# A list-scheduled graph-network kernel: GpSimd instructions wait for VectorE instructions that the plan puts ahead of them

## The chip, the cores and the metric

The kernel runs on one core of a Trainium2 chip, in float32 throughout. A core has five engines that run their own queues in order: TensorE (PE in the profile, its weight loads PEld), VectorE (DVE), ScalarE (ACT), GpSimd (POOL) and SyncE (SP), which here issues all DMAs. [...] The metric is the device time of one execution in microseconds; a profile's span is the time between the first and last instruction of the profiled execution.

## The reference

128 graphs of 128 nodes with 512 features go through four layers. Each layer adds its result to its input and normalises every row. `adj` is a 128x128 matrix for each graph.

```python
x = layernorm(x + relu(An @ x @ W0 + b0))                    # layer 0; An = dh * (adj + I) * dh
q, k = split(x @ Wqk.T);  v = x @ Wv.T                       # layer 1
w = softmax_over_nodes(sum((q @ k.T) / 8 * adj, -1))
x = layernorm(x + w * v)
agg = adj @ x / max(deg, 1e-6)                               # layer 2
x = layernorm(x + relu(concat(x, agg) @ W2.T))
x = layernorm(x + An @ (x @ W3 + b3))                        # layer 3
```

`dh` is the inverse root of a row sum of `adj + I`, and `deg` a row sum of `adj`.

## The kernel before, in words

Four graphs make a tile (`G = 4`), so there are 32 tiles; the four layers of a tile are spread over several rounds of the main loop, so that at any time layer 0 of one tile, layer 1 of the same, and layers 2 and 3 of the tile before are in work (lines 889 to 905). `begin` (line 856) holds the first rounds, with the weights' sums between them, and lines 907 to 916 the last tile, in pairs of graphs.

Each 512x512 product (`project`, line 526; `l1_out`, line 729) is cut into two by two blocks and computed with seven block products instead of eight: B11, T1, B21, T2, B22, T3, T4. The left operands of T1, T2, B22 and T3 are sums of blocks, which `left_sums` (line 503) computes with four instructions of 128x512: s1, s2, the overwritten block a21, and s4. In the profile these are agg0s, agg2s, agg3s, xT1s, xT2s and, for a21, agg or xT. They run on GpSimd, but for some of `begin`. TensorE's products read them.

VectorE adds the products in PSUM to blocks in SBUF (u_o, s_o, v) and to `x`, takes the rows' means and variances (bno, mvo; bnv, mvv), prepares the adjacency of a later tile (deg, dh, ana, anT), and computes layer 1's scores: `l1_scores` (line 695) ends with four scr instructions, which give w; `l1_softmax` turns w on TensorE (p_w), takes the exponentials on ScalarE (e), scales them on VectorE, and turns them back (p_ws). `norm_stats` (line 626) sends mean and variance through GpSimd (rstd, with a power, then mr) and ScalarE (nmr, then x in place). The last norm is `norm_last` (line 601). Turned copies of x (xT1, xT2) go through DRAM and a VectorE transpose in the steady tiles, and over TensorE (p_xT, from xT1y or xT2y) in the first and last.

None of this is emitted where it is written. `Recorder` turns each call into an `Op` of a `Plan`, with a duration from `estimate` (line 292). `schedule` (line 197) then simulates the five engines: TensorE's order is the recorded one; each other engine takes, of its ready ops, the one whose latest allowed start is smallest. An op with `port` set (all of GpSimd's, and VectorE's with two large SBUF inputs, lines 303 to 308) may not start before the previous op with `port` has ended (lines 236 and 250). `emit` (line 268) then issues all ops in the planned order. That order binds each engine's own queue. Between two engines only the data's own dependencies become semaphore waits; the planned order of a GpSimd and a VectorE op with `port` is otherwise not enforced.

All instructions of the plan carry line 271 in the profile, so they are told apart by their tiles' names.

Of the kernel before, what the change touches and what calls it, by code (L numbers as in the profile page):

```python
# [32 lines left out]
class Ref:  # L33


    def __init__(self, tile_, steps, idx, quads):
        self.tile, self.steps, self.idx, self.quads = tile_, steps, idx, quads
# [83 lines left out]
class Op:  # L121
    def __init__(self, engine):
        self.engine, self.dur, self.lat, self.size, self.port, self.calls, self.preds, self.succs = engine, 0, 0, 0, False, [], set(), []
        self.last, self.start, self.end = float("inf"), None, None


class Plan:
# [2 lines left out]

    ENGINES = ("tensor", "vector", "scalar", "gpsimd", "sync")
    HOP = 200
    LAND, FLIGHT = 1600, 9
    HEAD, BUS = 40000, (62, 95)

    def __init__(self, nc, est):
        self.nc, self.est, self.ops, self.tags, self.group, self.dram = nc, est, [], {}, None, None
        for e in self.ENGINES:  # L140
            setattr(self, e, Recorder(self, e))

# [54 lines left out]
    def schedule(self):  # L197
        number = {op: i for i, op in enumerate(self.ops)}
        for (_, tag, bufs), tiles in self.tags.items():
            used = []  # L200
            for t in sorted((t for t in tiles if t.ops), key=lambda t: number[t.ops[0]]):
                if len(used) == bufs:
                    old = used.pop(min(range(bufs), key=lambda i: number[used[i].ops[-1]]))
                    assert number[old.ops[-1]] < number[t.ops[0]], (tag, bufs)
                    for op in t.ops:
                        if op.preds.isdisjoint(t.ops):
                            op.preds.update(old.ops)
                used.append(t)
        now = 0
        for op in self.ops:  # L210
            assert all(number[p] < number[op] for p in op.preds)
            for p in op.preds:
                p.succs.append(op)
            if op.engine == "tensor":
                op.last = now
                now += op.dur
        for op in reversed(self.ops):
            due = min([s.last - self.hop(op, s) for s in op.succs], default=now)
            op.last = min(op.last, due - op.dur)
        queue = {e: [] for e in self.ENGINES}  # L220
        waiting = {op: len(op.preds) for op in self.ops}
        free, bus, port = dict.fromkeys(self.ENGINES, 0), 0, 0
        pe = [op for op in self.ops if op.engine == "tensor"]
        for op in self.ops:
            if not op.preds:
                queue[op.engine].append((0, number[op], op))
        done, landed = [], []
        while len(done) < len(self.ops):
            best = None
            for e in self.ENGINES:  # L230
                q = queue[e]
                if e == "tensor":
                    q = [c for c in q if c[2] is pe[0]]
                if not q:
                    continue
                q = [(max(c[0], port if c[2].port else 0),) + c[1:] for c in q]
                at = max(free[e], min(c[0] for c in q))
                pick = min((c for c in q if c[0] <= at), key=lambda c: (c[2].last, c[1]))
                for c in q:
                    if at < c[0] < at + pick[2].dur and c[2].last < at + pick[2].dur and c[2].last < pick[2].last:  # L240
                        pick, at = c, c[0]
                if best is None or at < best[0]:
                    best = at, e, pick[2]
            at, e, op = best
            queue[e] = [c for c in queue[e] if c[2] is not op]
            if e == "sync" and len(landed) >= self.FLIGHT:
                at = max(at, landed[-self.FLIGHT])
            op.start, op.end = at, at + op.dur
            free[e] = op.end
            if op.port:  # L250
                port = op.end
            if e == "sync":
                bus = max(bus, op.end + self.LAND) + op.size / self.BUS[at > self.HEAD]
                op.lat = max(op.lat, bus - op.end)
                landed.append(op.end + op.lat)
            if e == "tensor":
                pe.pop(0)
            done.append(op)
            for s in op.succs:
                waiting[s] -= 1  # L260
                if not waiting[s]:
                    queue[s.engine].append((max(p.end + self.hop(p, s) for p in s.preds), number[s], s))
        return done

    def hop(self, p, s):
        return p.lat if p.engine == s.engine and p.engine != "sync" else p.lat + self.HOP

    def emit(self):
        for op in self.schedule():
            for method, args, kw in op.calls:  # L270
                getattr(getattr(self.nc, op.engine), method)(  # L271
                    *[v.real() if isinstance(v, Ref) else v for v in args],
                    **{k: v.real() if isinstance(v, Ref) else v for k, v in kw.items()})


class Recorder:
# [35 lines left out]
def kernel(  # L312
# [10 lines left out]
    b3: bass.AP,  # L323
    out: bass.AP,
):
    nc = Plan(tc.nc, estimate)
    B = x.shape[0]
    NT = B // G
    last = NT - 1
# [55 lines left out]
    p = ps_t.tile([P, C, P], FP, tag="pt", name="p_warm")  # L385
# [563 lines left out]
```

## Time and profile before

| | |
|---|---|
| time, median of 4 runs | 2452.12 us (2450.71 to 2452.63) |
| profiled execution: its own time, its span | 2451.62 us, 2449.8 us |
| granted TensorE clock over the span | 1.0 |
| TensorE busy (matmul; weight load) | 2438.0 us; 2090.9 us |
| VectorE, ScalarE, GpSimd busy | 1715.1 us; 995.5 us; 1314.5 us |
| distance of one tile to the next, from 194 to 2237 us | 75.6 us |
| a left sum on GpSimd, 128x512 (xT1s) | 1.27 us |
| rstd's power on GpSimd, 128x2 (rstdo) | 0.72 us |

A group of instructions is named by the tile that it writes and the tiles that it reads; `128x512 f32 x31` is the shape and the count. A row of the groups gives busy time and mean ns of one, then the engine's idle time before them and what ended it. A row of the waits gives the sum in us, how often, and the longest. A row of the timeline gives start and duration in us; in brackets stands the idle time before it and its releaser. "issue" means that the profile shows nothing that the engine waited for.

### The profile page before, as it was taken

To read this page: it belongs to the slowest core of one execution; us is meant where nothing else is said; L and a number is where in the kernel's file an instruction comes from. 1 tells how busy PE (TensorE), PEld (TensorE's weight loads), DVE (VectorE), ACT (ScalarE), POOL (GpSimd) and SP (SyncE) were. 2 spreads that over 40 slices of the span, in tenths; PEclk is the share of its full clock that TensorE was granted. 3 is DMA by queue.
4 is the path that set the end of the run, shared out by engine and by line. 5 is a ranking of instruction groups with operands and counts; after the bars stand their busy time and mean duration, and the time that the engine had idled before them with its cause. 6 is when DMAs were issued, how large, how long until landed. Compare 5 with 4: busy or idle time off the path is not lost.

```text
span 2449.8 us, 35470 instructions
## 1 busy us (share of the span) xinstructions
PE 2438.0 (100%) x12462; PEld 2090.9 (85%) x12462; DVE 1715.1 (70%) x3396; ACT 995.5 (41%) x2117; POOL 1314.5 (54%) x1580
## 2 busy tenths in 40 slices
PE   9999999999999999999999999999999999999998
PEld 8888888888888888888888888888888888888887
DVE  7767766677666777667776667767677676777666
ACT  4334343443434444344443444333444334443345
POOL 6464555555555555555455554645546455555543
PEclk9999999999999999999999999999999999999999
DMA  5133233442424423244332443233442333433220
GB/s 181 48 99 104 73 108 91 125 125 58 115 78 125 125 67 110 77 122 125 82 96 82 117 125 104 73 99 104 121 123 63 96 103 117 125 74 96 67 80 35
DMA packets 393266, 241.15 MB, mean 98 GB/s; under 512 B 140416, under 2 KB 358016, under 8 KB 393088
## 3 DMA queue, kind: packets, MB, share of 16 engines
q1 hardware_dynamic: 393088, 238.88, 35.3%
q8 instruction: 99, 1.62, 0.3%
q14 instruction: 79, 0.65, 0.1%
HBM read 126.62 MB, written 112.20 MB: 97 GB/s over the span
## 4 chain that ended last, share of the span: by engine, by line
PE 98%; DVE 1%; POOL 0%; issue 0%; ACT 0%; POOLq 0%; DVEq 0%
PE p_o L271 63%; PE p_v L271 20%; PE p_agg L271 14%; PE p_sc L271 1%; PE p_w L271 0%; DVE x L271 0%; PE p_warm L271 0%; PE p_ws L271 0%; PE p_xT L271 0%; DVE u_o L271 0%; POOL xT1s L271 0%; POOL rstdo L271 0%; POOL w2x_sb L271 0%; DVE ana L271 0%; DVE bno L271 0%
## 5 line engine op out<-in xcount | busy, mean ns | idle before, releaser
L271 PE MATMUL p_o<-w_sb,agg 128*128 128x256 f32 x2048 | 471.4, 380 | 0.9 <-DVE u_o L271 0.9
L271 PEld LDWEIGHTS p_o<-w_sb,agg 128*128 128x128 f32 x2048 | 386.8, 190 | 52.1 <-DVE u_o L271 0.9
L271 ACT COPY agg<-p_agg 128x512 f32<-128x512 f32 (+1 forms) x415 | 226.0, 552 | 407.3 <-PE p_agg L271 407.1
L271 PE MATMUL p_v<-wv_sb,xT 128*128 128x320 f32 x1024 | 291.7, 433 | 0.1
L271 PE MATMUL p_o<-w2x_sb,xT 128*128 128x256 f32 x1024 | 263.1, 380 | 1.0 <-ACT xT L271 1.0
L271 DVE TENSOR_TENSOR v<-p_v,v 128x320 f32<-128x320 f32 x316 | 154.4, 489 | 155.9 <-PE p_v L271 155.4
L271 PE MATMUL p_o<-w2a_sb,agg 128*128 128x256 f32 x1024 | 262.9, 379 | 0.0
L271 PEld LDWEIGHTS p_v<-wv_sb,xT 128*128 128x128 f32 x1024 | 192.3, 190 | 76.3 <-ACT xT L271 0.6
L271 PEld LDWEIGHTS p_agg<-anT,x 128*128 128x128 f32 x2048 | 238.8, 192 | 7.0 <-DVE anT L271 0.6
L271 DVE TENSOR_TENSOR u_o<-p_o,u_o 128x512 f32<-128x512 f32 (+1 forms) x196 | 129.2, 671 | 162.0 <-PE p_o L271 160.4
L271 PE MATMUL p_agg<-anT,x 128*128 128x128 f32 x2048 | 239.4, 275 | 0.3 <-DVE anT L271 0.3
L271 PEld LDWEIGHTS p_o<-w2x_sb,xT 128*128 128x128 f32 x1024 | 194.5, 190 | 30.5 <-ACT xT L271 1.4
L271 PE MATMUL p_v<-wv_sb,xT1s 128*128 128x320 f32 x768 | 217.6, 433 | 1.1 <-POOL xT1s L271 1.1
L271 PEld LDWEIGHTS p_o<-w2a_sb,agg 128*128 128x128 f32 x1024 | 194.9, 190 | 26.1
L271 POOL TENSOR_SCALAR rstdo<-mvo 128x2 f32<-128x2 f32 (+1 forms) x131 | 35.7, 273 | 321.2 <-DVE mvo L271 318.8
L271 PE MATMUL p_o<-w2x_sb,xT2s 128*128 128x256 f32 x768 | 197.2, 379 | 0.0
L271 PE MATMUL p_o<-w2a_sb,agg2s 128*128 128x256 f32 x768 | 197.2, 379 | 0.0
L271 ACT ACTIVATE x<-x,nmro,rstdo 128x512 f32<-128x512 f32 x256 | 195.0, 807 | 3.4
L271 PEld LDWEIGHTS p_v<-wv_sb,xT1s 128*128 128x128 f32 x768 | 145.8, 190 | 58.9 <-POOL xT1s L271 2.0
L271 PE MATMUL p_o<-w_sb,agg0s 128*128 128x256 f32 x768 | 180.9, 380 | 0.0
L271 PE MATMUL p_o<-w_sb,agg3s 128*128 128x256 f32 x744 | 173.9, 384 | 0.0
L271 DVE BATCH_NORM_STATS2 bno<-x 128x6 f32<-128x512 f32 x258 | 170.4, 683 | 3.9
(146 smaller groups left out, 4256.9 us busy)
## 6 DMA issues: line engine op xcount, KB each, us to landing
x<-in_x_dram SPq DMA_DIRECT2D x31, 1024.0 KB, 6.6
out_dram<-x SPq DMA_DIRECT2D x31, 1024.0 KB, 5.2
xT2s<-x SPq DMA_DIRECT2D x120, 256.0 KB, 2.8
xT2y<-xT2s SPq DMA_DIRECT2D x240, 128.0 KB, 2.7
xT1s<-x SPq DMA_DIRECT2D x120, 256.0 KB, 2.5
xT1y<-xT1s SPq DMA_DIRECT2D x240, 128.0 KB, 3.1
sa<-ana SPq DMA_DIRECT2D x120, 128.0 KB, 3.1
ya<-sa SPq DMA_DIRECT2D x120, 128.0 KB, 3.2
```

The source lines that it names most:

```text
L271: getattr(getattr(self.nc, op.engine), method)(*[v.real() if isinstance(v, Ref) else v for v in args], **{k: v.real() if isinstance(v, Ref ...
```

## The change

When `schedule` places a GpSimd op (all of them have `port`), and the last op with `port` that it placed is VectorE's, and the GpSimd op's own inputs would be ready earlier than 500 ns after that VectorE op's planned end, the GpSimd op gets `after` set to the VectorE op. `emit` then adds a dependency, so that the last instruction of the GpSimd op waits on a semaphore for the last instruction of the VectorE op. The plan's times and its order are computed as before. The plan keeps the tile context (`tc`) for this.

```diff
@@ class Op
-        self.last, self.start, self.end = float("inf"), None, None
+        self.last, self.start, self.end, self.after = float("inf"), None, None, None
@@ class Plan
-    HOP = 200
+    HOP, CLOSE = 200, 500
...
-    def __init__(self, nc, est):
-        self.nc, self.est, self.ops, self.tags, self.group, self.dram = nc, est, [], {}, None, None
+    def __init__(self, tc, est):
+        self.tc, self.nc, self.est, self.ops, self.tags, self.group, self.dram = tc, tc.nc, est, [], {}, None, None
@@ schedule
-        free, bus, port = dict.fromkeys(self.ENGINES, 0), 0, 0
+        free, bus, port, owner = dict.fromkeys(self.ENGINES, 0), 0, 0, None
...
             if op.port:
-                port = op.end
+                ready = max((p.end + self.hop(p, op) for p in op.preds), default=0)
+                if e == "gpsimd" and owner is not None and owner.engine == "vector" and ready < port + self.CLOSE:
+                    op.after = owner
+                port, owner = op.end, op
@@ emit
-                getattr(getattr(self.nc, op.engine), method)(
+                op.ins = getattr(getattr(self.nc, op.engine), method)(
                     *[v.real() if isinstance(v, Ref) else v for v in args],
-                    **{k: v.real() if isinstance(v, Ref) else v for k, v in kw.items()})
+                    **{k: v.real() if isinstance(v, Ref) else v for k, v in kw.items()}).ins
+            if op.after is not None:
+                self.tc.add_manual_dep(op.ins, op.after.ins.name, mybir.DependencyInfo(
+                    mybir.DependencyClass.Sync, mybir.DependencyReason.DATA))
...
-    nc = Plan(tc.nc, estimate)
+    nc = Plan(tc, estimate)
```

## The prediction

> **What bounds the kernel now.** I read the page first: busy shares, then the chain that ended last.
>
> ```profile
> span 2449.8 us, 35470 instructions
> PE 2438.0 (100%) x12462; PEld 2090.9 (85%) x12462; DVE 1715.1 (70%) x3396; ACT 995.5 (41%) x2117; POOL 1314.5 (54%) x1580
> PE 98%; DVE 1%; POOL 0%; issue 0%; ACT 0%; POOLq 0%; DVEq 0%
> ```
>
> TensorE is the bound from end to end; GpSimd is half idle. So the change can only gain where TensorE waits, and only lose where a later GpSimd result makes TensorE wait. Next I read who waited for whom on TensorE. The matmul side waited under 5 us in all. The weight-load side shows two repeated gaps without a named releaser:
>
> ```profile
> PEld p_ws L271 <- issue: 10.7, 32, 0.4
> PEld p_w L271 <- issue: 9.6, 27, 0.4
> ```
>
> The timeline of weight loads tells them apart. A usual tile, then the second-last:
>
> ```profile
> 1251.52 1.60 PEld L271 LDWEIGHTS p_o<-w_sb,agg 128*128 128x128 f32 x8
> 1253.47 0.08 PEld L271 LDWEIGHTS p_w<-ident,w 128*4 128x4 f32 x1 [0.35 <-issue]
> 1253.50 0.30 PEld L271 LDWEIGHTS p_o<-w_sb,agg3s 128*128 128x128 f32 x2
> ```
>
> ```profile
> 2310.41 1.60 PEld L271 LDWEIGHTS p_o<-w_sb,agg 128*128 128x128 f32 x8
> 2312.03 0.09 PEld L271 LDWEIGHTS p_w<-ident,w 128*4 128x4 f32 x1
> 2312.25 0.52 PEld L271 LDWEIGHTS p_o<-w_sb,agg3s 128*128 128x128 f32 x3
> ```
>
> From the eight loads' start to the agg3s load is 1.98 us in the first and 1.84 us in the second. So the p_w gap is a real stall worth some 0.14 us, of which TensorE makes good the rest (0.33 lost, 0.19 recovered). The p_ws gap is there in every tile, and e has been ready 0.4 to 0.8 us by then: that one is TensorE's own. What p_w waits for stands on VectorE and GpSimd in the same microseconds:
>
> ```profile
> 1250.70 1.28 POOL L271 TENSOR_TENSOR agg3s<-agg 128x512 f32<-128x512 f32 x1 [5.70 <-ACT agg L271]
> ```
>
> ```profile
> 1250.78 1.75 DVE L271 TENSOR_TENSOR ana<-ana,d 128x512 f32<-128x512 f32 x1
> 1252.46 0.27 DVE L271 SCALAR_TENSOR_TENSOR scr<-p_sc,dmn,v 128x64 f32<-128x64 f32 x1
> 1253.28 0.08 DVE L271 DVE_READ_ACCUMULATOR scr<-p_sc,dmn,v 128x1 f32 x1
> ```
>
> The last scr ends at 1253.35, and p_w loads 0.12 us later; that distance is the same in 28 tiles (27 in the row above, one under another releaser). scr is late because ana in front of it takes 1.75 us. The groups by form show what it costs otherwise:
>
> ```profile
> L271 DVE TENSOR_TENSOR ana<-ana,d 128x512 f32<-128x512 f32 x32 | 36.9, 1154 | 1.2 <-POOL d L271 1.2
> L271 DVE TENSOR_TENSOR ana<-ana,rdeg 128x512 f32<-128x512 f32 x32 | 22.8, 712 | 0.1
> ```
>
> **What the skill says.** The Trainium skill, "SBUF — State Buffer", section "Who interferes with whom": a VectorE instruction with two SBUF inputs contends with a GpSimd instruction that reads SBUF, and whoever issues first holds the shared pair for its whole instruction. The trace agrees: GpSimd started 0.08 us ahead and VectorE's 0.7 us became 1.75. The same section says TensorE and ScalarE wait on no one; TensorE's products kept their spacing through both spans. "Perfetto Trace Analysis", section "GPSIMD Engine Instruction", warns that GpSimd's spans are unreliable; here successive starts of left sums are 1.34 to 1.37 us apart with spans of 1.27, so I use the spans and add 0.08 between.
>
> **The change, part by part.** (1) No instruction moves on any of the five queues, DMAs included. The planner's arithmetic for starts is the same; only `after` and its waits are new. (2) In the emitted program 344 GpSimd instructions wait for a later VectorE instruction than before. Laid on the trace, 56 of these VectorE instructions had ended before GpSimd started, so those waits cost nothing; 288 had not, with ends 0.05 to 5 us after GpSimd's start, half of them 1 to 2 us. (3) GpSimd gets 110 more semaphore instructions, where two waits meet. No row prices one. I take nothing; bound: not below nothing, and up to one GpSimd hop, 0.08 us, each, 9 us in all on an engine that idles 1135 us.
>
> What matters is how late GpSimd's results come against how early they are needed. I followed each result through its consumers to the TensorE product it feeds, taking the idle time on the way as its slack.
>
> *Steady tiles, the gain.* agg3s<-agg now goes behind ana. ana runs 1250.78 to 1251.49 (0.71), about 1.0 us earlier than now. The first scr then starts when p_sc is done (1251.77), the fourth ends at 1252.66, and p_w may load at 1252.78; TensorE gets there at 1253.14. The stall is gone: 28 tiles by 0.145 us (load to load around p_w, 0.760 + 0.033 us with the stall, 0.432 + 0.216 in the four tiles without) = **4.0 us gained**.
>
> *Steady tiles, the delays.* agg3s<-agg starts at 1251.58 (a VectorE end reaches GpSimd in 0.09), 0.88 us late, ends at 1252.86; its product now comes at 1253.36: 0.45 us to spare. Behind it on the queue, agg<-agg waits for ana<-ana,rdeg: it ends at about 1259.2 instead of 1256.7, 2.5 late with 3.9 of slack. rs<-rs,d is 3 late with 8 of slack. rstdv, which feeds ScalarE's normalisation and then the transposing DMAs on SyncE, ends 1.3 to 2.1 late with 2.1 to 2.9 of slack: some 0.75 to spare. In turn the late agg<-agg blocks one x<-v,ws,x until 1259.2; VectorE's next reading of p_o is then 0.2 late with 0.55 of slack. Before agg3s, and again before xT1s, GpSimd idles for microseconds, so a delay doesn't pass into the next tile. Cost: nothing, under cover of 0.45 us or more. Were the cover gone, each 0.1 us would cost 3 us over 30 tiles.
>
> *Opening.* Slack is small here:
>
> ```profile
> 33.40 1.26 POOL L271 TENSOR_TENSOR agg<-agg 128x512 f32<-128x512 f32 x1
> 36.18 0.29 POOL L271 TENSOR_TENSOR mro<-mvo,rstdo 128x2 f32<-128x2 f32 x1
> 45.68 1.26 POOL L271 TENSOR_TENSOR xT1s<-xT 128x512 f32<-128x512 f32 x1
> ```
>
> ```profile
> 36.50 0.20 ACT L271 ACTIVATE nmro<-mro 128x2 f32<-128x2 f32 x1 [6.63 <-POOL mro L271]
> 38.16 1.12 ACT L271 COPY xT1y<-x 128x512 f32<-128x512 f32 x2
> ```
>
> The agg<-agg here waits for x<-s_o,x, now ending at 35.9: it runs 36.0 to 37.3, and the three rstdo/mro steps behind it end at 38.6 instead of 36.5: 2.2 late, slack 0.46. So p_xT<-xT1y stalls TensorE 1.7 us. Later steps catch up in part: w2x_sb behind s_o delays xT1s only from 45.68 to some 46.7, and TensorE, which waited 0.66 us there already, resumes at 48.0 instead of 47.0. **1.0 us lost.** From there the opening's chains run relative to TensorE again.
>
> *End.* mrv<-mvv,rstdv (2392.55) waits for four x<-v,ws,x: 1.0 late with no slack, but TensorE's 0.68 us wait five steps on (xT, 2397.5) takes most of it: 0.3 lost. agg30s moves x<-s_o,x by 0.2. The last left sums queue behind x<-s_o,x, agg31s ending at 39.8 instead of 39.2 with 0.2 of slack: 0.35. **Some 0.8 us lost.**
>
> Sum against the profiled execution's own time, 2451.6 (span 2449.8): −4.0 + 1.0 + 0.8 = −2.2, so 2449.4. That execution lies 0.5 below the median shown; against the median I put **2450.0 us**. What a measurement of this kernel can tell from no change is about 0.2%, 4.9 us: 2447.2 to 2457.0.
>
> **Rivals.** *A, slower: the wait takes the place of the stall.* If VectorE's long ana is not shortened by going first, agg3s<-agg starts at 1252.62 and is usable at 1253.95, against 1253.50: 0.45 us on 30 tiles, 13.5 us, and with 1.8 for the ends 2467. It decides from a GpSimd delay of 1.33 us at this one place. For it: GpSimd's queue is in order, and rstdv has little more cover. Against: 0.71 for ana<-ana,rdeg. A half miss, say rstdv 0.2 short on 30 tiles, gives 2456 to 2460. *B, faster: the ends gain too.* VectorE is blocked twice by 1 us in the opening (1.68 for x<-u_o,x at 33.54), and TensorE's opening waits come to some 2 us. If VectorE's earlier ends outweigh GpSimd's delays, 4.0 + 2 gives 2446. Against: mro, not VectorE, is named as ScalarE's releaser. *C, nothing:* p_w's gap is TensorE's turn to a transpose, as at p_ws; then only the ends' 1.8 remain, 2453.9. Against: tiles without the gap. *D, the change doesn't act:* the waits are already met. 288 of 344 are not.
>
> **How the numbers follow.** Forecast (with C and D, whose times also lie within 0.2%) 0.70: its own range 2447.5 to 2454.5. A and half misses 0.17; B 0.13. The range takes most of B and the smaller misses, and leaves out full A and what lies below 2445: 2445 to 2459. Faster 0.13, same 0.70, slower 0.17.
>
> **What would show it.** Right: ana<-ana,d and ana<-ana,ident near 0.7 us; p_w's "issue" wait gone; agg3s named as waiting for VectorE, not ScalarE; p_xT stalling about 1.7 us near 39.5; tiles 75.49 us apart instead of 75.64. Wrong: TensorE waiting for POOL agg3s or for ScalarE's x in every tile (A), or an opening shorter than now (B).

## The result, and the profile after

The changed kernel takes 2448.94 us (median of 41 runs, 2447.94 to 2450.19), the kernel before beside it 2451.98 us (61 runs, 2450.59 to 2453.93). The ratio is 0.9987, with a 95% interval of 0.9983 to 0.9992: 3.0 us, 0.13%, where 2.2 us were forecast. The page's head and its chain of work that ended last:

```profile
span 2447.3 us, 35580 instructions
PE 2434.4 (99%) x12462; PEld 2092.5 (86%) x12462; DVE 1671.2 (68%) x3396; ACT 999.2 (41%) x2117; POOL 1229.5 (50%) x1580
PE 96%; DMA 1%; POOL 1%; DVE 1%; ACT 1%; SPq 0%; issue 0%; POOLq 0%; DVEq 0%; ACTq 0%
```

TensorE still sets the end, and the span is 2.5 us shorter. VectorE and GpSimd shed 44 and 85 us of busy time. Both engines idle so much that hardly any of this reaches the span. What reached it is in the waits of TensorE's weight loads (sum in us, times, longest):

```profile
PEld p_ws L275 <- issue: 10.7, 32, 0.4
PEld p_xT L275 <- ACT xT1y L275: 2.7, 3, 1.9
PEld p_agg L275 <- ACT x L275: 1.3, 1, 1.3
PEld p_v L275 <- POOL xT1s L275: 1.3, 3, 0.5
PEld p_o L275 <- POOL agg31s L275: 0.4, 1, 0.4
```

The p_w row is gone. Three waits are longer than before: p_xT (0.5 before), p_agg (0.3) and agg31s (no row). In a usual tile the weight loads now run through p_w without a gap; GpSimd's first left sum of agg3s, and VectorE beside it, stand in the next two fences (timeline of the same microseconds):

```profile
1249.87 1.60 PEld L275 LDWEIGHTS p_o<-w_sb,agg 128*128 128x128 f32 x8
1251.50 0.09 PEld L275 LDWEIGHTS p_w<-ident,w 128*4 128x4 f32 x1
1251.71 1.60 PEld L275 LDWEIGHTS p_o<-w_sb,agg3s 128*128 128x128 f32 x8
```

```profile
1249.96 1.27 POOL L275 TENSOR_TENSOR agg3s<-agg 128x512 f32<-128x512 f32 x1 [6.81 <-ACT agg L275]
```

```profile
1249.13 0.69 DVE L275 TENSOR_TENSOR ana<-ana,d 128x512 f32<-128x512 f32 x1
1250.13 0.28 DVE L275 SCALAR_TENSOR_TENSOR scr<-p_sc,dmn,v 128x64 f32<-128x64 f32 x1 [0.31 <-PE p_sc L275]
...
1250.96 0.08 DVE L275 DVE_READ_ACCUMULATOR scr<-p_sc,dmn,v 128x1 f32 x1
```

From the eight loads' start to the agg3s load is 1.84 us, as in the tiles without the stall before. ana runs ahead of agg3s and takes 0.69 us instead of 1.75; agg3s starts 0.14 us after ana's end. The profile still names ScalarE's agg as what released it. The first scr now waits for TensorE's p_sc, so VectorE has time left. agg3s ends at 1251.23 and its product's load comes at 1251.71: with 0.05 us from a GpSimd end to a load that waits for it (seen in the runs below where this load waits), 0.43 us are left to spare. Groups by form:

```profile
L275 DVE TENSOR_TENSOR ana<-ana,d 128x512 f32<-128x512 f32 x32 | 21.9, 684 | 1.8 <-POOL d L275 1.7
L275 DVE TENSOR_TENSOR ana<-ana,ident 128x512 f32<-128x512 f32 x32 | 22.1, 691 | 0.0
L275 DVE TENSOR_TENSOR ana<-ana,rdeg 128x512 f32<-128x512 f32 x32 | 24.0, 750 | 0.1
L275 DVE TENSOR_SCALAR e<-e,rsum 4x128 f32<-4x128 f32 x32 | 18.2, 568 | 1.1
L275 POOL TENSOR_TENSOR agg<-agg 128x512 f32<-128x512 f32 x92 | 116.9, 1270 | 30.2 <-DVE x L275 19.2 <-DVE ana L275 10.4 <-PE p_o L275 0.7
```

ana<-ana,d fell from 1154 to 684 ns. In every second tile it is ana<-ana,ident that stands beside agg3s, and it fell from 1152 to 691. Each mean of before mixes 14 blocked instructions of some 1.76 us with others of 0.68. e<-e,rsum fell from 1171 to 568: it took 1.11 and 1.35 us in turn from tile to tile, and takes 0.27 and 0.94. The left sum on GpSimd fell from 1352 to 1270: the engine that had been blocked was not always VectorE. In the opening, on GpSimd and then on ScalarE:

```profile
34.15 1.27 POOL L275 TENSOR_TENSOR agg0s<-agg,agg0s 128x512 f32<-128x512 f32 x1 [1.15 <-DVE x L275]
36.04 1.27 POOL L275 TENSOR_TENSOR agg<-agg 128x512 f32<-128x512 f32 x1 [0.63 <-DVE x L275]
...
38.38 0.20 POOL L275 TENSOR_TENSOR mro<-mvo,rstdo 128x2 f32<-128x2 f32 x1
...
45.98 1.27 POOL L275 TENSOR_TENSOR xT1s<-xT 128x512 f32<-128x512 f32 x1 [0.80 <-ACT xT L275]
```

```profile
38.61 0.20 ACT L275 ACTIVATE nmro<-mro 128x2 f32<-128x2 f32 x1 [8.96 <-POOL mro L275]
...
40.28 1.12 ACT L275 COPY xT1y<-x 128x512 f32<-128x512 f32 x2
```

mro ends 2.1 us later than before, so ScalarE's xT1y does too, and TensorE waits for it. But xT1s is only 0.30 us later. At the end, in the last tile (weight loads):

```profile
2391.56 1.86 PEld L275 LDWEIGHTS p_agg<-arT,x 128*128 128x128 f32 x16 [1.34 <-ACT x L275]
...
2394.72 0.73 PEld L275 LDWEIGHTS p_o<-w2x_sb,xT 128*128 128x128 f32 x4 [0.47 <-ACT xT L275]
```

The first wait was 0.27 us before, the second 0.91.

**Where the time went.** I matched the 12462 weight loads of both profiled executions one for one and took the difference of their starts. It changes at few places:

| place | TensorE's shift, us |
|---|---|
| p_w in 28 tiles: −0.327, then +0.183 at the load after it | −4.06 |
| opening: p_xT +1.72 and p_v<-xT1s −0.93, some smaller ones −0.16 | +0.63 |
| end: p_agg +1.08, p_o<-w2x,xT −0.44, agg31s +0.30 and small ones | +0.97 |
| p_v<-xT1s in single tiles: −0.38 at 780, +0.37 at 1007, +0.20 at 1310 | +0.19 |
| sum | −2.3 |

The rest of the span's 2.5 us is that TensorE's warm-up loads (p_warm), which begin at 1.34 us in both, end 0.17 us earlier. In the other profiles the loads at 9 us stand from 0.6 us earlier to 0.3 later than in the kernel before. The opening's +0.63 holds against this one execution of the kernel before; what others do there is told with the runs side by side.

### The profile page after: what moved, and what is told of

Its sections match the earlier page's. It is cut to its first block, busy times and chain, and to the rows that moved or that the text cites. A ratio compares the mean times of both kernels' runs of the same rounds, so it can differ in the third digit from the quotient of the medians.

```text
span 2447.3 us, 35580 instructions
## 1 busy us (share of the span) xinstructions
PE 2434.4 (99%) x12462; PEld 2092.5 (86%) x12462; DVE 1671.2 (68%) x3396; ACT 999.2 (41%) x2117; POOL 1229.5 (50%) x1580
## 4 chain that ended last, share of the span: by engine, by line
PE 96%; DMA 1%; POOL 1%; DVE 1%; ACT 1%; SPq 0%; issue 0%; POOLq 0%; DVEq 0%; ACTq 0%
PE p_o L275 61%; PE p_v L275 20%; PE p_agg L275 14%; PE p_sc L275 1%; SPq L275 0%; DMA xT1y<-xT1s 0%; DMA xT1s<-x 0%; ACT x L275 0%; DVE x L275 0%; PE p_warm L275 0%; PE p_ws L275 0%; PE p_xT L275 0%; POOL xT2s L275 0%; DMA xT2y<-xT2s 0%; DVE xT L275 0%
## 5 line engine op out<-in xcount | busy, mean ns | idle before, releaser
L275 ACT ACTIVATE nmro<-mro 128x2 f32<-128x2 f32 (+1 forms) x130 | 26.5, 204 | 367.6 <-POOL mro L275 367.4
```

The lines of the kernel that those rows point to most:

```text
L275: op.ins = getattr(getattr(self.nc, op.engine), method)(*[v.real() if isinstance(v, Ref) else v for v in args], **{k: v.real() if isinstan ...
```

## The experiments

The theory is the prediction's: the p_w stall goes because agg3s<-agg no longer blocks ana<-ana,d; the other waits only cost, at the two ends. Rival 1: VectorE is freer everywhere, and agg3s is only one of many causes. Rival 2: agg3s has no real cover, and the result is luck of a small delay. All kernels keep the order of every engine's own instructions, but for GpSimd's emission against the others in the two kernels with a moved wait.

**Only the wait at agg3s.** 30 of the 344 waits are left; `label` gives the name of the tile that an op writes.

```diff
-            if op.after is not None:
+            if op.after is not None and self.label(op).startswith("agg3s1_"):
```

> Only the 30 waits of the first left sum of agg3 are kept; the other 314 are dropped. Theory (the whole gain is TensorE's wait for w at p_w, 28 tiles by 0.145 us, and the other waits only cost, in the opening and at the end): 4.0 us under the kernel before, ratio 0.9984, a span near 2445.8; p_w without a stall; no stall of p_xT near 39.5; agg3s usable 0.4 us ahead of its product. Rival (VectorE runs freer everywhere, and that pays): the other waits carry part of the gain, so this kernel gains clearly less than 3 us, ratio 0.9990 or above.

Measured: 2447.24 us (16 runs) against 2451.78 of the kernel before; ratio 0.9981 (0.9973 to 0.9988), span 2445.5 us. The p_w row is gone, and the ends' waits are those of before:

```profile
PEld p_xT L279 <- ACT xT1y L279: 0.5, 1, 0.5
PEld p_agg L279 <- ACT x L279: 0.3, 1, 0.3
```

Thirty waits carry the gain, with p_w's two shifts (−0.328 and +0.183) in the same tiles.

**All waits but that one.** The same line with `not`; 314 waits.

> All 314 waits but those 30. Theory: ana<-ana,d and ana<-ana,ident stay at 1.15 us mean, p_w keeps its stall in 28 tiles, and only the losses remain: 0.6 us in the opening and 1.0 us at the end, so 1.5 us over the kernel before, ratio 1.0006, span near 2451.4. Rival (VectorE freer everywhere): this kernel is still faster than before, ratio 0.9990 to 0.9995.

Measured: 2452.63 us (13 runs); ratio 1.0004 (0.9996 to 1.0013), span 2450.4 us. The waits of its weight loads:

```profile
PEld p_w L279 <- issue: 9.6, 27, 0.4
PEld p_xT L279 <- ACT xT1y L279: 2.7, 3, 1.9
PEld p_agg L279 <- ACT x L279: 1.3, 1, 1.3
```

The p_w stall is the kernel before's, to the digit, and so is ana<-ana,d at 1154 ns, though e<-e,rsum fell to 807. In the steady tiles rival 1 falls: what VectorE gains elsewhere in them is worth nothing. The 0.9 us over the kernel before, where 1.5 were expected, can't be told from none.

**Only the steady tiles, and only the ends.** `inner` holds the ops recorded in the loop before its last turn; the second kernel has `not in`.

```diff
-            if op.after is not None:
+            if op.after is not None and op in self.inner:
...
+    nc.low = len(nc.ops)
...
+        if t == last:
+            nc.inner = set(nc.ops[nc.low:])
```

> The waits of the steady tiles alone (303), none in the opening and none in the last round. Theory: the same as the agg3 waits alone, 4.0 us under the kernel before, ratio 0.9984: the 273 other steady waits are covered and neither gain nor cost. If the two tiles where xT1s held TensorE up for 0.2 to 0.4 us come from these waits, they are in this trace too and it is some 0.6 us worse. Rival (freer VectorE): better than the agg3 waits alone by 1 us or more.

> Only the 41 waits of the opening and the last round; the 303 of the steady tiles are dropped. Theory: p_w keeps its stall, p_xT near 39.5 stalls 1.7 us of which 0.6 is left by 80 us, the last round loses 1.0: 1.5 us over the kernel before, ratio 1.0006, span 2451.3. Rival (the ends are free): ratio 1.0000.

Measured: the steady tiles alone 2448.1 us (21 runs; ratio 0.9984, 0.9977 to 0.9990; span 2444.9), the ends alone 2452.8 us (13 runs; ratio 1.0005, 0.9997 to 1.0014; span 2451.8). The p_xT and p_agg waits stand in the second only (2.7 and 1.3 us). That the ends lose something is seen in the traces (+0.64 opening, +0.93 end there, against the one profile of the kernel before); the medians alone can't tell it from zero. The steady tiles alone came out 0.9 us above agg3s's wait alone on the same chip, where no difference was expected. The weight loads show no regular shift but p_w's in either, so this stays unexplained; it says how far two such medians can lie apart.

**agg3s<-agg later still.** It waits for the second scr of the same round, then for the fourth, and GpSimd's ops in between are emitted after it; the second kernel has `[3]` where the first, shown, has `[1]`. All other waits are left out, so these stand against the kernel with agg3s's wait alone.

```diff
+        for s1 in [op for op in ops if self.label(op).startswith("agg3s1_")]:
+            s1.after = scr[f"scr_{int(self.label(s1)[7:]) + 1}"][1] 
```

> The agg3 wait alone, set on the second scr. The wait on the fourth scr delayed the sum by 1.22 us against p_w and cost 0.79 us a tile, so the cover was 0.43. Here the sum starts some 0.75 us later than behind ana. Theory (cover 0.43, then one for one): 0.32 us by 30 tiles, 9.7 us over the agg3 wait on ana, some 2457, ratio 1.002. If a late sum costs only once it passes another limit, less: 2447 to 2450.

> The agg3 wait alone, but set on the fourth scr of the tile instead of on ana; nothing else waits. In the changed kernel's trace the fourth scr ends at 1251.03 where agg3s<-agg starts at 1249.96: the sum starts 1.16 us later, is usable at 1252.44, and its product's weights, loaded at 1251.71, come 0.73 us late, of which the next load makes good 0.11. Theory (cover at this place is 0.43 us): 0.62 us by 30 tiles, 18.6 us over the kernel with the agg3 wait on ana, so some 2466.5 us, ratio 1.006; TensorE waits for POOL agg3s in 30 tiles. If the sum's lateness is absorbed elsewhere: like the agg3 wait alone, 2448.

Measured: 2459.59 us (5 runs; ratio 1.0031, 1.0019 to 1.0044) and 2471.08 us (5 runs; ratio 1.008, 1.0066 to 1.0094), that is 12.0 us over the second run of agg3s's wait alone (2447.64, below) and 23.8 over the first, each from the same chip. GpSimd and the weight loads of a tile with the second scr:

```profile
1255.97 1.26 POOL L294 TENSOR_TENSOR agg3s<-agg 128x512 f32<-128x512 f32 x1 [7.55 <-DVE scr L294]
```

```profile
1256.69 0.09 PEld L294 LDWEIGHTS p_w<-ident,w 128*4 128x4 f32 x1
1257.28 1.59 PEld L294 LDWEIGHTS p_o<-w_sb,agg3s 128*128 128x128 f32 x8 [0.51 <-POOL agg3s L294]
```

And with the fourth:

```profile
1260.91 1.26 POOL L294 TENSOR_TENSOR agg3s<-agg 128x512 f32<-128x512 f32 x1 [8.11 <-DVE rs L294]
```

```profile
1261.23 0.09 PEld L294 LDWEIGHTS p_w<-ident,w 128*4 128x4 f32 x1
1262.23 1.59 PEld L294 LDWEIGHTS p_o<-w_sb,agg3s 128*128 128x128 f32 x8 [0.91 <-POOL agg3s L294]
```

Take p_w's load as the clock. In the changed kernel agg3s<-agg starts 1.54 us ahead of it and the product is loaded 0.21 after it. In these two the start is 0.72 and 0.32 us ahead, so 0.82 and 1.22 later; the product's load is at 0.59 and 1.00, so 0.38 and 0.79 later. In both 0.43 to 0.44 us were covered and the rest came through in full. Over 30 tiles that is 11.4 and 23.7 us, which the medians repeat (another 0.44 us came in either at the last tile's p_o<-w_sb,agg). The expectations were some 2 and 5 us low: they let TensorE make up 0.11 us of each stall at its next load, and it makes up nothing. Rival 2 falls: the cover is real, and so is the cliff behind it.

**Both kernels once more, side by side.** No edit.

> The changed kernel once more, on the same chip as the next three, to set it beside the agg3 wait alone. Theory (the ends cost 0.6 us in the opening and 1.0 us in the last round): 1.5 us slower than the agg3 wait alone, some 2448.8 against 2447.3. Rival (all waits but agg3's are free): no difference. Stalls of TensorE for xT1s, 0.2 to 0.9 us in one or two tiles, stood in other tiles in each profile so far, with and without waits: if they are the DMAs' chance, this profile has them in other tiles than the first one of this kernel (1007 and 1310 us).

> The agg3 wait alone, beside the changed kernel on one chip. Theory: 4.0 to 4.5 us under the kernel before, 1.5 us under the changed kernel. Rival: equal to the changed kernel.

Measured: the changed kernel 2448.64 us (21 runs; ratio 0.9988, 0.9981 to 0.9995), agg3s's wait alone 2447.64 us (19 runs; ratio 0.9984, 0.9977 to 0.9990), the kernel before 2451.66. The intervals of the two overlap. agg3s's wait alone has the lower median, by 1.0 us here (1.5 expected) and by 1.5 in the first runs, each against its own kernel before. That fits what the traces show at the end, 0.97 us; by the medians alone it is no more than the unexplained 0.9 between two kernels above.

The opening does not account for it, as these two traces show. Without the waits there, VectorE is blocked twice by GpSimd ahead of u_o, for which a load of TensorE waits (VectorE, GpSimd and the weight loads of agg3s's wait alone):

```profile
14.68 1.76 DVE L279 TENSOR_TENSOR w_sb<-w_sb 128x512 f32<-128x512 f32 x1
16.36 1.82 DVE L279 TENSOR_TENSOR agg0s<-agg0s,agg 128x256 f32<-128x256 f32 x2
```

```profile
14.49 1.39 POOL L279 TENSOR_TENSOR sb_o<-s_o,b_sb 128x512 f32<-128x512 f32 x1 [3.06 <-ACT s_o L279]
15.96 1.60 POOL L279 TENSOR_TENSOR s_o<-s_o,b_sb 128x512 f32<-128x512 f32 x1
```

```profile
20.70 1.38 PEld L279 LDWEIGHTS p_o<-w_sb,agg0s 128*128 128x128 f32 x7 [1.18 <-DVE u_o L279]
```

In the changed kernel these two rows of VectorE take 0.68 and 0.75 us, sb_o starts behind the last agg0s, and the load doesn't wait. All six profiles without waits in the opening have this stall, of 0.18 (the kernel before), 0.19, 0.46, 0.78, 1.18 and 1.21 us; none of the seven with them, all or most, has it. From the warm-up to 80 us the changed kernel's two profiles lose 0.63 us each against the kernel before's; the six without waits there lose 0.0 to 1.2, 0.50 in the mean. So the opening's waits lose 1.7 us at p_xT, gain at p_v and here, and cost some 0.13 us on average, an estimate from these few profiles. The prediction left out the gain here.

The spans scatter by more than I had thought. Executions of these two kernels, near 1984 us, show why; VectorE's transposition and GpSimd's first sum behind it, first in agg3s's wait alone:

```profile
1984.27 1.30 DVE L279 STREAM_TRANSPOSE xT<-xT1y 128x512 f32<-128x512 f32 x2 [3.71 <-DMA xT1y<-xT1s]
```

```profile
1985.72 1.26 POOL L279 TENSOR_TENSOR xT1s<-xT 128x512 f32<-128x512 f32 x1 [3.79 <-DVE xT L279]
```

and in the changed kernel:

```profile
1983.51 1.30 DVE L275 STREAM_TRANSPOSE xT<-xT1y 128x512 f32<-128x512 f32 x2 [2.90 <-DMA xT1y<-xT1s]
```

```profile
1984.96 1.27 POOL L275 TENSOR_TENSOR xT1s<-xT 128x512 f32<-128x512 f32 x1 [2.97 <-DVE xT L275]
```

The turning DMA of one tile landed 0.76 us later in one execution, and the TensorE load behind it stalled 0.51 us. Each profile has none to three of such stalls, in tiles that change (the changed kernel's second profile has one, at 2066 us, where its first had none): the two executions of the changed kernel, one program, differ by 0.85 us in their sum of shifts through them alone. In which tile they fall I can't predict, and why the DMA was late wasn't tried.

**Which wait makes the opening late.** The prediction put it on agg<-agg alone. All 344 waits are kept but the one at the opening's agg<-agg; then but the one at the agg0s sum ahead of it; then but both and the last tile's mrv<-mvv,rstdv.

```diff
-            if op.after is not None:
+            if op.after is not None and self.label(op) not in ("agg0_1", "agg0s4_1", "mrv_31_0"):
```

> All waits of the change but that of the opening's agg<-agg for x<-s_o,x (343 of 344 kept). By the prediction's step this wait alone makes the opening late: without it agg<-agg follows the agg0s sum in front of it, mro ends near its time before, and TensorE's wait in the row p_xT<-xT1y is back at 0.5 us in all (after: 2.7). Rival: the waits in front of it already make it late (in the changed kernel the last agg0s sum starts 2.6 us later than before, at 34.15, behind x<-u_o,x). Then agg<-agg can start no sooner than 35.4, mro ends 0.1 to 0.6 us earlier than in the changed kernel (38.58), and the row still shows 2.0 us or more. Time within 0.6 us of the changed kernel either way.

> All waits of the change but that of the opening's last agg0s sum for x<-u_o,x. By the prediction's step nothing changes: agg<-agg still waits for x<-s_o,x, which ends near 35.9, so it starts near 36.0 and the row p_xT<-xT1y stays at some 2.7 us. If the lateness came from the agg0s sum alone, the row falls to 0.5 us.

> All waits of the change but three: those of the opening's last agg0s sum and agg<-agg, and that of the last tile's mrv<-mvv,rstdv for x<-v,ws,x. If these three carry the losses: the agg0s sum starts near 33.1, mro ends near 37.0 (0.5 us later than before, which the 0.46 us to spare cover), the row p_xT<-xT1y shows 0.5 to 0.7 us instead of 2.7, the row p_agg<-x 0.3 instead of 1.3, agg31s stays at 0.4. The opening's 0.57 and the end's 0.64 us come back, and xT1s may start up to 0.4 us earlier than before: 2447.5 us (2447.0 to 2448.0), ratio 0.9983, the time of the kernel with the wait at agg3s alone. If other waits carry them, it stays at 2448.7.

Measured: 2448.47 us and 2448.6 us (one run each), and 2447.9 us without the three (20 runs; ratio 0.9986, 0.9979 to 0.9993; the kernel before 2451.52). The p_xT row in the three, in that order:

```profile
PEld p_xT L279 <- ACT xT1y L279: 2.5, 3, 1.7
```

```profile
PEld p_xT L279 <- ACT xT1y L279: 2.7, 3, 1.9
```

```profile
PEld p_xT L279 <- ACT xT1y L279: 1.7, 3, 1.0
PEld p_agg L279 <- ACT x L279: 0.3, 1, 0.3
```

Taking out agg<-agg's wait shortens TensorE's wait by 0.2 us and agg0s's by nothing: each is enough to make the opening late. Without both the row falls to 1.7 us, with a longest wait of 1.0, where 0.5 to 0.7 in all was expected. GpSimd in that kernel:

```profile
33.91 1.73 POOL L279 TENSOR_TENSOR agg<-agg 128x512 f32<-128x512 f32 x1
35.60 0.66 POOL L279 TENSOR_SCALAR rstdo<-mvo 128x2 f32<-128x2 f32 x1
```

The two overlap with VectorE again and take 1.73 and 0.66 us, against 1.27 and 0.23 in the changed kernel. So a removed wait brings a collision back. And the agg0s sum, behind waits that were left in, still starts 1.1 us later than before (32.68 against 31.58). The opening's loss fell from 0.63 to 0.33 us by the shifts (against the same profile of the kernel before), and the mrv wait gave back its 0.64 in full. The time came out within the range expected, though through less at one place.

## Why the prediction was right, and where it was off

**The gain: right in place, mechanism and size.** 28 tiles by 0.145 us, 4.06 against 4.0; the tiles are 75.49 us apart now and were 75.64, as named in advance. Only agg3s's wait brings it, and without that wait it stays away. The scr, not ana, is what p_w waited for, and the first scr is bound by p_sc now, as foreseen. This refutes rival C (the gap belongs to TensorE) and D (the change doesn't act).

**The cover of agg3s: right.** 0.45 us forecast, 0.43 measured. Rival A did not come, and its point of decision, a delay of 1.33 us, is confirmed: measured from the start of the eight loads, agg3s is 0.91 us later than before (0.82 ahead of it then, 0.09 behind it now; 0.88 forecast), and with the cover of 0.43 that makes 1.34. Its price past that point, one for one, is what the two moved waits show. One reading behind it was too narrow: left sums start 1.34 to 1.37 us apart only where one reads the other's result. In the kernel before, agg<-agg starts 1.23 us after the agg3s in front of it (1254.97 against 1253.74), which has a span of 1.27, so these spans overlap a little. No term of the sum rests on it.

**The delays behind agg3s: hidden, as said.** agg<-agg ends 4.89 us after the agg3s load (1256.60 against 1251.71) instead of 3.2 before: 1.7 late, not 2.5. e<-e,rsum takes 0.27 us in that tile, so ana<-ana,rdeg, which agg<-agg waits for, came earlier. No weight load waits for rstdv longer than before.

**The opening: the stall was right, its cost was mis-sized.** The p_xT stall was 1.72 us, 1.7 in the forecast, and mro's end lay 0.02 us from the forecast. The step that failed is the catching up: "delays xT1s only from 45.68 to some 46.7", so that TensorE resumes 1.0 us late. xT1s started at 45.98, and the opening lost 0.63. I had carried over durations from before for the steps in front of xT1s. But GpSimd had been blocked in them: rstdo's two steps took 0.67 and 1.02 us, and take 0.21 and 0.71 now; w2x_sb took 1.74 and takes 1.28. A wait that ends an overlap shortens the instruction that waits, too. So GpSimd was free early, and xT1s then waited 0.80 us for ScalarE's xT, which was late because of the p_xT stall. A second term was left out: the opening's waits take away the stall at the agg0s load near 20 us. In the profile of the kernel before that stall is 0.18 us, of which 0.05 stayed; in others it is up to 1.2. Also, agg<-agg's wait was named as the cause alone; the agg0s sum's wait in front of it would have done it by itself.

**The end: right within 0.2 us.** mrv's chain cost 1.08 and gave back 0.44, where 1.0 and 0.7 were forecast (so 0.64 net, not 0.3); agg31s cost 0.30 against 0.35. The mis-sized term is the 0.68 us wait at xT: it gave back only what ScalarE's later copy of xT left of it. A separate 0.2 us for agg30s did not show. In all 0.97 against 0.8.

**Rival B** had the ends gain as well, through a VectorE that is blocked less. At one place it is so, the agg0s load near 20 us, which it did not name. On the whole the ends lose, as the ends' waits alone show (traces: +0.64 and +0.93 us), though the opening little on average.

**The sum.** −4.06 + 0.63 + 0.97 = −2.5 between these two executions, against −2.2 forecast; the opening was put too dear and the end too cheap, so the errors cancel in part. With the 0.13 us that the opening costs on average in place of 0.63, the sum is −3.0, which is the difference of the medians. That agreement is worth no more than half a microsecond: two executions of the same program differ by 0.85 us through single late DMAs, which the forecast did not count. One sign named in the prediction failed: agg3s is hardly ever shown as waiting for VectorE's ana (once, 6.9 us). Most of its idle time stands in this row of the waits on GpSimd:

```profile
POOL agg3s L275 <- ACT agg L275: 220.2, 28, 9.8
```

The idle time before agg3s is microseconds long and put down to one event; the wait that was added shows in the start, 0.14 to 0.15 us behind ana's end in the tile shown and in the others with the gain.

## What to carry to other kernels

A wait that keeps one engine from overtaking another pays only where the overtaken instruction is on the path of the engine that bounds the kernel: here at one left sum of each tile, 30 waits of 344, and at one place of the opening. Before adding it, measure how much later the waiting result may come, for past that point each 0.1 us cost 3 us over the 30 tiles. And put it at such places alone: the last tile, where chains are short of slack, paid 1 us for the other waits, and the opening lost at p_xT more than it gained.

## What the runs showed of the hardware

- **The blocked engine can be either.** The Trainium skill, "SBUF — State Buffer", section "Who interferes with whom", says that whoever issues first holds the shared pair; so waits shorten GpSimd's work as well: agg<-agg 1352 to 1270 ns over 92 instructions, a 128x2 rstdo step in the opening 0.67 to 0.21 us.
- **A tiny VectorE instruction suffered most for its length.** e<-e,rsum, 4x128 with one tile and a column of scalars, took 1171 ns in the mean before. In the changed kernel it takes 0.27 us where it starts 0.07 us ahead of a left sum on GpSimd, and 0.94 us in the tiles where the left sum started 0.4 us ahead of it. The same section says that tensor_scalar can enter a mode that contends with GpSimd, and the trace agrees with it.
- **How much TensorE makes good depends on what stood still.** Of a p_w stall of 0.33 us it recovered 0.18 at the next load. Of an agg3s stall of 0.38 or 0.79 us, right behind p_w, it recovered nothing.
- **Semaphore instructions on a half idle GpSimd cost nothing that shows.** The changed kernel has 80 instructions more than agg3s's wait alone (35580 against 35500), and its steady tiles are as long, 75.49 us: the p_w shifts are the only regular ones in either.
